# A decoder's block transposes by way of DRAM: one VectorE operation per 512 columns, 8 KB tiles, 2 KB stores, paired loads

## The chip, the core and the metric

The kernel runs on one core of a Trainium2 chip. The metric is the device time of one execution in microseconds (us), as the median of several runs. The engines are TensorE (PE; its weight loads, PEld, overlap the matmuls), VectorE (DVE), ScalarE (ACT), GpSimd (POOL) and SyncE (SP), which issues nearly all DMAs. SBUF is the on-chip memory with 128 partitions; PSUM holds the results of matmuls; DRAM is the memory outside.

## The reference

Six blocks are added to a residual stream `x` of 4 batches x 512 tokens x 512 features, each on the layernorm of `x`:

```python
x = x + L0_attn(layernorm(x))           # 16 heads of 32, one shared key and value head
x = x + L0_xattn(layernorm(x), ctx)     # mixes features with softmax(q k^T) of the context
x = x + L0_ffn(layernorm(x))            # 4-bit weights, width 1408, SiLU gate, then RMS norm
x = x + L1_attn(layernorm(x))           # 16 heads of 32
x = x + L1_xattn(layernorm(x), ctx)     # 16 heads of 128, 8 key/value heads, 512 keys
x = x + L1_ffn(layernorm(x))            # 32 slots of rank 16, the top 2 are gated
```

`L1_xattn` is the part that the change touches most. For each batch and head:

```python
scores = q @ k.T / sqrt(128)            # 512 x 512
attn   = softmax(where(mask, scores, -inf))
out    = attn @ v                       # then all heads' outputs times Wo
```

All is float32. The kernel keeps that precision with three matmuls of a high and a low part for each product (`three`): a value is split into a rounded `h` tile and the rest, an `l` tile.

## The kernel before

The stages follow one another, each with its own period: L0 (attention), X0 (mixing), FF, L1 (attention), X1 (cross-attention, 64 heads) and R1 (the routed part). Later stages' loads and layernorms begin while earlier stages run.

No instruction is issued as it is written. `Recorder` notes every operation as a task with the tiles that it reads and writes; `put` and `after` give it a place in a rough order. Then `arrange` (line 327) plans all tasks with `run`, a list scheduler that has a cost for each operation, DMA queues, PSUM banks and numbered buffers for every pool. It goes forward and backward `ROUNDS` times, and of the `ROUNDS + 1` forward plans keeps the shortest by its own costs. Some tasks may go to either of two engines: `split_sbuf` (line 704) puts the rounded copy on ScalarE or VectorE and the subtraction on GpSimd or VectorE, and `run` decides which. The instructions are then issued in the planned order, all from line 1845, and each engine keeps its order. So all profile rows of the planned work have L1845, and only the tiles' names tell them apart.

Two pools of SBUF matter here. `tp_` holds `TBUFS` = 50 tiles of 2 KB per partition (tag `t`), `wp` holds `WBUFS` = 17 tiles of 4 KB (tag `w`), for weights and for stacked operands.

`block_turn(tiles, got)` (line 756) transposes a matrix of 512 x 512 that lies in four tiles of 128 x 512. It has three parts:

- `turn(t)`: VectorE transposes tile `t` in blocks of 32 x 32 (`tr<-pe` in X1, `tr<-h` for layernorms). It takes two operations of 256 columns, each into one of two 4 KB tiles `tr` from `wp`.
- `away(j)`: SP stores half `j`, in four DMAs of 32 partitions, to a DRAM buffer `turn` (`turn<-tr`). The pieces are 512 bytes long.
- `back(k)`: SP loads one chunk of 128 columns, 256 KB, in pieces of 2 KB, into a tile `pt` of `tp_` (`pt<-turn`), and `split_sbuf` makes `turnedh` and `turnedl` from it for TensorE.

In X1 each of the 64 heads makes its scores with TensorE (`kTh`, `qh` and the like), VectorE moves them out of PSUM with the mask and their row minimum (`pe`, `nmc`), ScalarE takes the exponential, `pe` is scaled, `block_turn` turns the four `pe` tiles, and TensorE weighs the values with `turnedh` and `turnedl` (`vh`, `vl`). The same helper turns the normalised `h` tiles of 15 layernorms: four each in FF, L1 and X1, three in R1. The others are transposed by TensorE.

The functions that the diff touches and what calls them:

Of the kernel before, what the change touches and what calls it, by code (L numbers as in the profile page):

```python
# [10 lines left out]
F32 = mybir.dt.float32  # L11
# [10 lines left out]
P = 128  # L22
NB = 4
S = 512
D = 512
QT = S // P
KC = D // P
NH = 16
HD = 32
HG = P // HD  # L30
# [7 lines left out]
LN_EPS = 1e-5  # L38
RMS_EPS = 1e-6
BIG = 1e30  # L40
TBUFS = 50
WBUFS = 17
START = 45.0
DQ = 50.0
PER_L0, PER_X0, PER_F1, PER_L1, PER_X1, PER_R1 = 16.5, 12.5, 6.1, 22.5, 11.7, 25.0
# [9 lines left out]
WG = 2  # L55
OUT1 = 3.0
UM, UE, UH, UL = 0, 0, 0, 0
ROUNDS = 16

KEEP = 0, 1, 0, 1, 1, 2  # L60
TRACE = []
# [7 lines left out]
DT = 6  # L69
# [257 lines left out]
def arrange(tasks):  # L327
# [8 lines left out]
    best = None  # L336
    for n in range(ROUNDS + 1):
        done = run(tasks, False)
        span = max(t.end for t in done)
        TRACE.append(round(span, 1))  # L340
        if best is None or span < best[0]:
            best = span, done, [(t.start, t.end, t.engine, t.calls) for t in done], [
                (tile, tile.slot) for t in done for tile in t.tiles
            ]
        if n == ROUNDS:
            break
# [202 lines left out]
def decoder_kernel(ctx: ExitStack, tc: tile.TileContext, a: dict, out: bass.AP):  # L549
# [8 lines left out]
    nc = Recorder()  # L558
    PSUM = bass.MemoryType.PSUM

    def pool(name, bufs, n=None, **k):
        return Pool_(ctx.enter_context(tc.tile_pool(name=name, bufs=bufs or 1, **k)), bufs, n or name)

    base = pool("base", None)
    small = pool("small", 4)
    wp = pool("weights", WBUFS)
    tp_ = pool("tiles", TBUFS)
    dram = pool("scratch", None, space=bass.MemoryType.DRAM)
    ps = pool("ps", 1, space=PSUM)

# [29 lines left out]
    n = 2 * NI * KC  # L600
# [31 lines left out]
    def T(dt=F32, shape=(P, S), name="t"):  # L632
        return tp_.tile(list(shape), dt, tag="t", name=name)

    def pair(shape=(P, S), name="p"):
        return T(F32R, shape, name + "h"), T(F32R, shape, name + "l")
# [19 lines left out]
    def at(pr, *ix):  # L656
        return pr[0][ix], pr[1][ix]
# [46 lines left out]
    def split_sbuf(pr, src, dt, act=False):  # L704
        hi, lo = pr
        after(dt, lambda: copy(hi, src, *(("scalar", "vector") if act else ("vector", "scalar"))))
        after(dt + 0.8, lambda: join(lo, src, f32(hi), ALU.subtract, "gpsimd", "vector"))
# [4 lines left out]
    def add_to_x(t, src):  # L712
        nc.vector.tensor_tensor(x[:, t, :], x[:, t, :], src, ALU.add)
# [16 lines left out]
    def weight(t, key, src, cols=None, keep=False):  # L730


        got = {}

        def load():
            if key in stored:
                got["w"] = wp.tile(stored[key].tile.shape, F32R, tag="w", name="w")
                nc.sync.dma_start(f32(got["w"]), f32(stored[key]))
            else:
                got["w"] = split_weight(key, src, cols, keep, act=ACT_JIT and keep)  # L740

        put(t, t, [load])
        if keep and key[0] in EARLY:
            early.append((key, src, cols))

        def parts(sl=ALL, flat=False):
            if flat:
                return got["w"][:, sl]
            return got["w"][:, 0, sl], got["w"][:, 1, sl]

        return parts

    def chunks(w):
        return w.rearrange("(c p) o -> p c o", p=P)

    def block_turn(tiles, got):


        tr, dr = [None] * 2, [None] * 2

        def turn(t):
            for j in range(2):
                if t == 0:
                    tr[j] = wp.tile([P, 2 * S], F32, tag="w", name="tr")
                nc.vector.transpose(
                    tr[j].rearrange("p (b t i) -> p b t i", t=QT, i=HD)[:, :, t, :],
                    tiles[t][:, j * 2 * P : (j + 1) * 2 * P].rearrange("p (b i) -> p b i", i=HD),
                )

        def away(j):  # L770
            dr[j] = dram.tile([2, P, HG, P], F32, tag="turn", name="turn", bufs=DT)
            for n in range(HG):
                nc.sync.dma_start(
                    dr[j][:, :, n, :].rearrange("c (q j) n -> j (c q) n", j=HD),
                    tr[j][n * HD : (n + 1) * HD, :].rearrange("j (b n) -> j b n", n=P),
                    run=4 * P,
                )

        def back(k):
            pt = T(name="pt")  # L780
            nc.sync.dma_start(pt, dr[k // 2][k % 2].rearrange("p a n -> p (a n)"))
            got[k] = pair(name="turned")
            split_sbuf(
                [g.rearrange("p (t a i) -> p a t i", t=QT, a=HG) for g in got[k]],
                pt.rearrange("p (a t i) -> p a t i", t=QT, a=HG),
                3.5,
                True,
            )

        return (  # L790
            [lambda t=t: turn(t) for t in range(QT)],
            [lambda j=j: away(j) for j in range(2)],
            [lambda k=k: back(k) for k in range(KC)],
        )

    def layernorm_T(t0, t1, b, on_act=0, blocks=False, pool=False):
# [44 lines left out]
        if blocks:  # L841
            turns, aways, backs = block_turn(st["h"], st["hT"])
            put(n, t1, turns)
            put(t1, t1 + 0.2, aways)
            put(t1 + 4, t1 + 5, backs)
        else:
            put(n, t1, [lambda c=c: turn(c) for c in range(KC)])
# [200 lines left out]
    for b in range(NB):  # L1048
        t0 = T_X0 + b * PER_A0
        cT = context(t0 - 6, b)  # L1050
        u = {"qk": [None] * 2, "at": [None] * QT}

        def both(pq, j, u=u, b=b):
            u["qk"][j] = pair(name="qk")
            split(u["qk"][j], pq, cols[:, 5 + j : 6 + j], 1.3, b < SP)

        for j in range(2):
# [3 lines left out]
                lambda k, j=j: wx(slice(k * 2 * P + j * P, k * 2 * P + (j + 1) * P)),  # L1061
                cT,
                CC,
                lambda pq, j=j, both=both: both(pq, j),
# [35 lines left out]
    for b in range(NB):  # L1100
# [27 lines left out]
        for c in range(KC):  # L1128
            t0 = now + (4 * b + c) * per
            u = {}  # L1130

            def queries(pq, u=u, c=c):
# [7 lines left out]
                lambda k, c=c: wq0[k](slice(c * P, (c + 1) * P)),  # L1140
# [255 lines left out]
    for i in range(NI):  # L1396
        t = DQ + (ff0 + NI * per - 45 - DQ) * i / NI
# [12 lines left out]
    for b in range(NB):  # L1410
# [23 lines left out]
        for k in range(QT):  # L1434
# [5 lines left out]
                lambda c, k=k, hT=hT, wv=wv: (at(hT[c], ALL, tok(k)), wv[c]()),  # L1440
                lambda pv, k=k, f=values: f(pv, k),
            )
        oT = []
        for c in range(KC):
            t0 = now + (4 * b + c) * per
            u = {}
            for j in range(2):
                n0 = j * D + c * P
                w = weight(
                    t0 - (A1 + 0.5 - 0.2 * j) * per,  # L1450
                    ("qk1", j, c),
                    chunks(a["wqkv1"][:, n0 : n0 + P]),
                    KC,
                    keep=True,
                )

                def turned(pq, j=j, c=c, u=u):
# [13 lines left out]
                    lambda k, w=w: w(slice(k * P, (k + 1) * P)),  # L1471
# [5 lines left out]
            def normalise(w, pd, c=c, oT=oT):  # L1477
# [18 lines left out]
                lambda h, k, v=v, c=c: v[k][:, (4 * c + h) * HD : (4 * c + h + 1) * HD],  # L1496
# [10 lines left out]
        for t in range(QT):  # L1507
# [5 lines left out]
                lambda c, t=t, oT=oT, wo=wo: (at(oT[c], ALL, tok(t)), wo[c]()),  # L1513
                lambda po, t=t, b=b: add_to_x(b * QT + t, po),
# [6 lines left out]
    for b in range(NB):  # L1521
# [12 lines left out]
        for g in range(4):  # L1534
# [21 lines left out]
            for j in range(2):  # L1556
# [3 lines left out]
                    lambda k, j=j, wk=wk: wk(slice(k * 2 * XH + j * XH, k * 2 * XH + (j + 1) * XH)),  # L1560
                    cT,
                    CC,
                    lambda pk, j=j, f=keyed: f(pk, j),
# [21 lines left out]
            for i in range(4):  # L1585
# [9 lines left out]
                u = {"pe": [None] * QT, "pT": [None] * QT}  # L1595

                def queries(pq, u=u):
# [6 lines left out]
                    lambda k, w=wq: w(slice(k * P, (k + 1) * P)),  # L1604
# [21 lines left out]
                def scale(t, u=u):  # L1626
# [4 lines left out]
                    scaled_by(pe, pe, rec[:, t % 2 : t % 2 + 1], "vector", "scalar")  # L1631

                turns, aways, backs = block_turn(u["pe"], u["pT"])

                def weigh(k, u=u, kv=kv, i=i, oT=oT):
# [98 lines left out]
    for b in range(NB):  # L1734
        t0 = now + b * per
        hT = layernorm_T(t0 - 2.1 * per, t0 - 1.5 * per, b, NA["R1"], b in DV["R1"])
        u = {"gu": [None] * QT, "gT": [None] * KC}
# [193 lines left out]
```

## Time and profile before

| What | Value |
|---|---|
| Median of 3 runs | 2060.33 us (2054.5 to 2066.38) |
| The profiled execution: its own time | 2058.85 us |
| The profiled execution: its span | 2057.1 us |
| TensorE clock granted, mean | 0.993 |
| Busy: PE, DVE, ACT, POOL | 96%, 90%, 60%, 58% of the span |
| DMA on SP's queue | 349472 packets, 465.50 MB, 72.7% of 16 engines' span |
| Stores `turn<-tr` | 632, 128 KB each |
| Loads `pt<-turn` | 316, 256 KB each |
| VectorE transposes | 632 of 128 x 256 (512 of `pe`, 120 of `h`) |

The profile is one execution seen by the hardware profiler. A group of instructions is given with its tiles, its shape, its count, its busy time, the mean length of one in ns, and the engine's idle time just before them with what ended it. The chain of waits follows the work that ended last back to the start, at each step to what released it. SPq is SP's queue of DMA issues. The DMA share is the mean busy share of the 16 DMA engines.

### The profile page before, as it was taken

To read this page: it belongs to the slowest core of one execution; us is meant where nothing else is said; L and a number is where in the kernel's file an instruction comes from. 1 tells how busy PE (TensorE), PEld (TensorE's weight loads), DVE (VectorE), ACT (ScalarE), POOL (GpSimd) and SP (SyncE) were. 2 spreads that over 40 slices of the span, in tenths; PEclk is the share of its full clock that TensorE was granted. 3 is DMA by queue.
4 is the path that set the end of the run, shared out by engine and by line. 5 is a ranking of instruction groups with operands and counts; after the bars stand their busy time and mean duration, and the time that the engine had idled before them with its cause. 6 is when DMAs were issued, how large, how long until landed. Compare 5 with 4: busy or idle time off the path is not lost.

```text
span 2057.1 us, 31942 instructions
## 1 busy us (share of the span) xinstructions
PE 1984.3 (96%) x9728; PEld 1476.8 (72%) x9728; DVE 1848.7 (90%) x3645; ACT 1239.2 (60%) x2461; POOL 1195.0 (58%) x930
## 2 busy tenths in 40 slices
PE   7999999999999999999999999999999999999999
PEld 6755554778877856565656777787888777887677
DVE  8999998999999889898899898999999889998883
ACT  5876767467757355454546767676666557555520
POOL 5688889378777466867577445454454244233610
PEclk9999999999999999999999999999999999999999
DMA  7554444656758777777764889999999899988911
GB/s 254 198 187 149 144 159 145 232 185 231 261 171 296 222 229 240 211 243 221 222 169 141 246 236 272 288 288 294 299 299 304 246 307 292 317 255 247 273 60 58
DMA packets 350075, 467.57 MB, mean 227 GB/s; under 512 B 28944, under 2 KB 211472, under 8 KB 349904
## 3 DMA queue, kind: packets, MB, share of 16 engines
q1 hardware_dynamic: 349472, 465.50, 72.7%
q8 instruction: 77, 1.26, 0.3%
q14 instruction: 94, 0.77, 0.1%
q10 hardware_dynamic: 432, 0.04, 0.0%
HBM read 291.36 MB, written 173.93 MB: 226 GB/s over the span
## 4 chain that ended last, share of the span: by engine, by line
PE 65%; DVE 12%; DMA 12%; ACT 5%; issue 2%; SPq 2%; POOL 1%; ACTq 0%; DVEq 0%; POOLq 0%
PE mm L1845 65%; DMA pt<-turn 6%; DVE pe L1845 2%; SPq L1845 2%; DVE tr L1845 2%; DMA stack<-stack 2%; DVE nm L1845 2%; DMA turn<-tr 2%; ACT pT L1845 1%; DMA stack<-ql 1%; DVE x L1845 1%; ACT turnedh L1845 1%; ACT pe L1845 1%; DVE ol L1845 1%; DVE ql L1845 1%
## 5 line engine op out<-in xcount | busy, mean ns | idle before, releaser
L1845 POOL TENSOR_TENSOR turnedl<-pt,turnedh 128x512 fp32r<-128x512 f32 x249 | 328.8, 1334 | 407.2 <-ACT turnedh L1845 181.7
L1845 PE MATMUL mm<-turnedh,w 128*128 128x512 f32 x1120 | 414.6, 398 | 7.8 <-ACT turnedh L1845 3.0
L1845 DVE TENSOR_REDUCE nm<-mm 128x1 f32<-128x512 f32 x512 | 323.3, 678 | 35.3 <-PE mm L1845 34.5
L1845 PE MATMUL mm<-stack 96*128 96x512 f32 (+1 forms) x1024 | 325.8, 422 | 25.6 <-DMA stack<-stack 17.7
L1845 ACT ACTIVATE pT<-mm 128x512 f32<-128x512 f32 x512 | 273.2, 609 | 78.9 <-PE mm L1845 70.4
L1845 POOL TENSOR_TENSOR acc<-acc,pT 128x512 f32<-128x512 f32 x200 | 271.0, 1378 | 31.5 <-DVE acc L1845 12.6
L1845 PEld LDWEIGHTS mm<-stack 96*128 96x128 f32 (+1 forms) x1024 | 186.1, 192 | 140.5 <-issue 35.4
L1845 PE MATMUL mm<-turnedl,w 128*128 128x512 f32 x736 | 282.8, 394 | 1.2 <-POOL turnedl L1845 1.2
L1845 PEld LDWEIGHTS mm<-turnedh,w 128*128 128x128 f32 x1120 | 211.2, 189 | 65.7 <-ACT gu L1845 7.8
L1845 ACT ACTIVATE pe<-pe,nmc 128x512 f32<-128x512 f32 x256 | 184.6, 722 | 112.6 <-DVE nmc L1845 105.9
L1845 ACT CAST turnedh<-pt 128x512 fp32r<-128x512 f32 x291 | 176.5, 617 | 113.5 <-DMA pt<-turn 105.7
L1845 PE MATMUL mm<-w,oh 128*128 128x512 f32 x640 | 203.9, 391 | 5.6 <-ACT oh L1845 5.6
L1845 POOL TENSOR_TENSOR acc<-pT 128x512 f32<-128x512 f32 x118 | 155.6, 1333 | 77.2 <-ACT pT L1845 60.9
L1845 DVE STREAM_TRANSPOSE tr<-pe 128x256 f32<-128x256 f32 x512 | 198.3, 419 | 2.2 <-ACT pe L1845 2.0
L1845 DVE CUSTOM_DVE_ANT_0 pe<-mm,mb 128x512 f32<-128x512 f32 x256 | 169.7, 670 | 4.9 <-PE mm L1845 4.3
L1845 POOL TENSOR_TENSOR w<-ws,w 128x512 fp32r<-128x512 f32 x93 | 126.0, 1364 | 70.1 <-ACT w L1845 41.2
L1845 PEld LDWEIGHTS mm<-turnedl,w 128*128 128x128 f32 x736 | 139.1, 189 | 26.5 <-POOL turnedl L1845 2.7
L1845 ACT ACTIVATE gu<-mm,scales 128x512 f32<-128x512 f32 x173 | 113.5, 691 | 57.5 <-PE mm L1845 56.8
L1845 PEld LDWEIGHTS mm<-w,oh 128*128 128x128 f32 x640 | 118.9, 188 | 32.1 <-ACT oh L1845 8.0
L1845 POOL TENSOR_TENSOR gu<-gu 128x512 f32<-128x512 f32 x83 | 109.7, 1333 | 44.4 <-DVE gu L1845 33.0
L1845 DVE SCALAR_TENSOR_TENSOR gu<-mm,scales,gu 128x512 f32<-128x512 f32 x176 | 122.1, 738 | 2.4 <-PE mm L1845 2.3
L1845 PE MATMUL mm<-w,ol 128*128 128x512 f32 x320 | 123.7, 391 | 0.0
(235 smaller groups left out, 4543.9 us busy)
## 6 DMA issues: line engine op xcount, KB each, us to landing
turn<-tr SPq DMA_DIRECT2D x632, 128.0 KB
pt<-turn SPq DMA_DIRECT2D x316, 256.0 KB
w<-scr SPq DMA_DIRECT2D x148, 512.0 KB
stack<-stack SPq DMA_DIRECT2D x96, 384.0 KB
scr<-w SPq DMA_DIRECT2D x56, 512.0 KB
stack<-qh SPq DMA_DIRECT2D x96, 256.0 KB
w<-gu SPq DMA_DIRECT2D x44, 512.0 KB
w<-dn SPq DMA_DIRECT2D x44, 384.0 KB
```

What stands on the lines that cost most here:

```text
L1845: got = getattr(getattr(real, t.engine), name)(*[made(v) for v in a_], **{n: made(v) for n, v in k.items()})
```

## The change

`turn` makes one operation of 512 columns into one 8 KB tile `tr`, from a new pool `big` of two buffers. `away` stores it in four DMAs of 256 KB with pieces of 2 KB. `back` loads two chunks at a time, 512 KB in pieces of 1 KB, into a 4 KB tile of `wp`, and splits each chunk from its half. For the room of `big`, `tp_` goes to 44 tiles and `wp` to 16. `ROUNDS` goes from 16 to 32. `run=` tells the planner the length of the pieces. Every computed value stays the same.

```diff
-TBUFS = 50
-WBUFS = 17
+TBUFS = 44
+WBUFS = 16
+BBUFS = 2
...
-ROUNDS = 16
+ROUNDS = 32
...
+    big = pool("big", BBUFS)
...
     def block_turn(tiles, got):
-        tr, dr = [None] * 2, [None] * 2
+        u = {}
 
         def turn(t):
-            for j in range(2):
-                if t == 0:
-                    tr[j] = wp.tile([P, 2 * S], F32, tag="w", name="tr")
-                nc.vector.transpose(
-                    tr[j].rearrange("p (b t i) -> p b t i", t=QT, i=HD)[:, :, t, :],
-                    tiles[t][:, j * 2 * P : (j + 1) * 2 * P].rearrange("p (b i) -> p b i", i=HD),
+            if t == 0:
+                u["tr"] = big.tile([P, KC * S], F32, tag="b", name="tr")
+
+            nc.vector.transpose(
+                u["tr"].rearrange("p (e c t i) -> p c e t i", e=HG, c=KC, t=QT)[:, :, :, t, :],
+                tiles[t].rearrange("p (c e i) -> p c e i", c=KC, e=HG),
+            )
+
+        def away(n):
+            if n == 0:
+                u["dr"] = dram.tile([P, HG, KC * P], F32, tag="turn", name="turn", bufs=DT)
+            nc.sync.dma_start(
+                u["dr"][:, n, :].rearrange("(e j) s -> j e s", j=HD),
+                u["tr"][n * HD : (n + 1) * HD, :].rearrange("j (e s) -> j e s", e=HG),
+                run=4 * S,
+            )
+
+        def back(k):
+            if k % 2 == 0:
+                u["pt"] = wp.tile([P, HG, 2 * P], F32, tag="w", name="pt")
+                nc.sync.dma_start(
+                    u["pt"], u["dr"][:, :, k * P : (k + 2) * P], run=8 * P
                 )
-
-        def away(j):
-            dr[j] = dram.tile([2, P, HG, P], F32, tag="turn", name="turn", bufs=DT)
-            for n in range(HG):
-                nc.sync.dma_start(
-                    dr[j][:, :, n, :].rearrange("c (q j) n -> j (c q) n", j=HD),
-                    tr[j][n * HD : (n + 1) * HD, :].rearrange("j (b n) -> j b n", n=P),
-                    run=4 * P,
-                )
-
-        def back(k):
-            pt = T(name="pt")
-            nc.sync.dma_start(pt, dr[k // 2][k % 2].rearrange("p a n -> p (a n)"))
             got[k] = pair(name="turned")
             split_sbuf(
                 [g.rearrange("p (t a i) -> p a t i", t=QT, a=HG) for g in got[k]],
-                pt.rearrange("p (a t i) -> p a t i", t=QT, a=HG),
+                u["pt"][:, :, k % 2 * P : (k % 2 + 1) * P].rearrange("p a (t i) -> p a t i", t=QT),
                 3.5,
                 True,
             )
...
-            [lambda j=j: away(j) for j in range(2)],
+            [lambda n=n: away(n) for n in range(HG)],
```

## The prediction

> **What bounds the kernel now.** I read the whole page first, then the busy time by stage, the chain of waits, the groups by shape and the issuing queue. All work issued through the recorder carries the one line L1845, so I go by tile names. First the page's shares:
>
> ```profile
> span 2057.1 us, 31942 instructions
> PE 1984.3 (96%) x9728; PEld 1476.8 (72%) x9728; DVE 1848.7 (90%) x3645; ACT 1239.2 (60%) x2461; POOL 1195.0 (58%) x930
> ```
>
> TensorE is the bound as a mean; VectorE stands close behind. The changed helper, `block_turn`, works 64 times in the stage X1 (about 1110 to 1960 us) and 15 times for layernorms elsewhere, so X1 is read for itself (columns: stage, its length, then busy time and count of PE, PEld, DVE, ACT, POOL, the granted clock, the DMA share, GB/s):
>
> ```profile
> 1110.00:1960.00 850.00, 824.93 (x3731) 666.12 (x3728) 774.37 (x1880) 543.86 (x1144) 391.23 (x298) 1.00 0.92 276
> 1300.00:1500.00 200.00, 196.06 (x890) 159.21 (x889) 189.11 (x457) 137.46 (x290) 101.33 (x77) 1.00 0.97 296
> ```
>
> TensorE sits idle for 25 us of the 850, at full clock. Matmuls overlap, so busy time hides thin gaps. In the timeline two 128x512 matmuls in a row take 0.61 us where one takes 0.39, a step of 0.22 to 0.23; two 128x256 take 0.40 where one takes 0.28, a step of 0.12. The groups from 1150 to 1900 hold 2972 of the first and 347 of the second: 2972 x 0.226 + 347 x 0.115 = 712 us of 750. So 38 us of slack at most (less if records are missing): X1 can gain 25 to 40 us. The chain of waits, cut to X1, says where the slack lies:
>
> ```profile
> by line: PE mm L1845 51.6%; DMA pt<-turn 12.9%; DVE pe L1845 5.6%; SPq L1845 4.7%; DVE tr L1845 4.4%; DMA turn<-tr 4.2%; issue 2.9%; ACT pe L1845 1.8%; ACT turnedh L1845 1.8%; DVE turnedl L1845 1.0%; DVE x L1845 1.0%; POOL turnedl L1845 0.9
> ```
>
> The path of the turned blocks (transposes, store issues, stores, loads) holds 4.4 + 4.7 + 4.2 + 12.9 = 26% of the chain. One passage of it, in order of time (start, length, what):
>
> ```profile
> 1199.90 1.59 SPq L1845
> ...
> 1201.54 2.44 DMA turn<-tr
> ...
> 1204.17 3.22 DMA pt<-turn
> ...
> 1207.41 0.62 ACT turnedh L1845
> ```
>
> SP issues stores one behind the other, the last store lands, the load that waited for it lands, and the copies begin. The rows priced below:
>
> ```profile
> L1845 DVE STREAM_TRANSPOSE tr<-pe 128x256 f32<-128x256 f32 x512 | 198.3, 419 | 2.2 <-ACT pe L1845 2.0
> L1845 DVE TENSOR_TENSOR turnedl<-pt,turnedh 128x512 fp32r<-128x512 f32 x67 | 72.6, 1085 | 24.2 <-ACT turnedh L1845 21.5 <-DMA turn<-tr 1.3 <-issue 1.2
> L1845 ACT ACTIVATE pT<-mm 128x512 f32<-128x512 f32 x512 | 273.2, 609 | 78.9 <-PE mm L1845 70.4 <-DVE s L1845 6.8 <-ACT w L1845 0.3
> L1845 SPq DMA_DIRECT2D turn<-tr x632: 302/463/1592, 390.1 to 1954.1; - x158
> L1845 SPq DMA_DIRECT2D pt<-turn x316: 319/424/2095, 396.6 to 1957.2; - x158
> ```
>
> **The change, part by part.**
>
> *Transposes.* 632 of 128x256 become 316 of 128x512, a shape that the trace has not. Two of 419 ns are 838, the upper end. The scaled subtraction takes 460 ns on 128x256 and 740 on 128x512, so 256 more elements cost 280: 419 + 280 = 700, which I take; a TENSOR_REDUCE over 512 takes 678, the lower end. Gain 316 x 0.138 = 44 us of VectorE (0 to 50). On X1's chain the transposes are 4.4% x 850 = 37 us; 0.138/0.838 of that is -6.
>
> But the planner spends it again. The built program puts 113 subtractions `turnedl` on VectorE (67 before), 49 copies `turnedh` (25), and 142 scalings of `pe` (166): 46 x 1.085 + 24 x 0.613 - 24 x 0.668 = +49 us. VectorE as a whole is not relieved; GpSimd is, by 46 x 1.334 = 61 us it did not need.
>
> *Issues on SP.* Stores 632 to 316, loads 316 to 158. At 0.463 and 0.424 us that is 146 + 67 = 213 us less of issuing. In the built program a DMA also waits for the one that used its completion semaphore eight issues earlier, so fewer and larger DMAs wait less often. X1's chain has 4.7% x 850 = 40 us of SP; twelve issues per turn become six: -20 (-10 if half of these pieces are of weights).
>
> *Stores in 2 KB pieces.* Between 60 and 300 us, where the rows moved have mostly 2 KB and more, 161 GB/s took a share of 0.50: 20.1 bytes per ns and engine. From 1300 to 1500, 0.97 x 16 x 200 = 3104 engine-us moved 59.2 MB. Some 16 heads store 16.8 MB of it in 512 B pieces; the other 42.4 MB at 20.1 cost 2109, so the stores took 995, 17 bytes per ns. At the rate of the long rows they take 836: -16%, or 5% of the stage's DMA time. On the chain (4.2%, 36 us) that is -6 at best, against a last store of 256 KB instead of 128, 0.43 us more at 296 GB/s, on about a dozen landings: +5. I take 0.
>
> *Loads of two chunks, in 1 KB pieces.* No row moves mainly 1 KB pieces; they lie between the two rates, so loads get 0 to 18% dearer and the stage's DMA share changes by between -5 points and none. For the copies that wait, the first chunk of a pair lands with the second: 256 KB more, 0.86 us at 296 GB/s. X1's chain has 110 us of these landings, some 24 of 4 to 5 us. Were all first chunks: +21; were all last: 0. I take +10, the middle, since first and second chunks are equally many.
>
> The Trainium skill, "DMA: Bandwidth & Descriptors", section "Why small descriptors are slow (HBM only)", gives each packet about 3 cycles beside one per 32 bytes. By that (an estimate from the page) a byte in 512 B pieces costs 19/16, in 1 KB 35/32, in 2 KB 67/64 cycles: stores -12%, loads +4.5%, which would put the share near 0.95. The same page, "Anatomy of one DMA", says that the semaphore fires only when the last byte is confirmed; this speaks against the change, whose first load waits for the whole 1 MB where it waited for half. The trace's landing of 2.44 us behind the last store fits; no row splits it.
>
> *Two 8 KB buffers.* A new wait: the first transpose of a turn waits for the four stores of the turn before the last. In the built program mostly 20 to 35 VectorE instructions of X1 (850/1880 = 0.45 us each) lie between that turn's last transpose and this one, 9 to 16 us; four issues and a landing are 4 x 0.46 + 2.4 to 5 = 4 to 7 us. So it is covered: 0. With the cover gone, the score evictions `pe<-mm` queue behind the transpose, their PSUM banks stay full and TensorE stops: at 1 us for each of 64 turns, 64 us.
>
> *Pools.* Six 2 KB tiles and one weight buffer fewer. In X1 the turned chunks leave the tile pool, so little is lost. From 60 to 1100 us TensorE idles 240 - 237.2 + 800 - 770.9 = 32 us; I price 12% fewer tiles at 12% more idle, +4, of the bounds 0 and +32 (idle doubled). X1's -16 is 0.25 us a turn; the eight layernorm turns there give back -2.
>
> *32 passes.* The planner keeps the best of 33 plans, not 17; every engine's order changes throughout. No row prices that: -10 to +10, taken as 0.
>
> Sum: -6 - 20 + 0 + 10 + 4 - 2 = -14 us; the parts' ends in X1 reach from -6 - 20 - 6 = -32 to -6 - 10 + 5 + 21 = +10. The profiled execution took 2058.85 us (span 2057.1), the median of the three runs is 2060.33, 1.5 more. From the median: 2046 us, with 2028 to 2050 as that case's own range. What comes next when the path shortens is TensorE itself, 25 to 40 us below.
>
> **Rivals.**
>
> *Nothing gained.* The turn path shortens at the issues and lengthens at the landings, and VectorE, as busy as before (91% in X1), sets the pace. For it: the 49 us given back, and DVE `pe` with 5.6% of X1's chain. Also, in the built order the matmuls between a head's last score and its first weighing grow from 24.4 to 27.1 us of steps: the planner found the turn longer, not shorter. Against: SP's part is certain. -6 - 10 + 0 + 10 + 4 = about -2: 2058.
>
> *Slower: the smaller tile pool.* X0, L0, FF and L1 run half the span and hardly use the turn, but plan with 44 tiles. Where a writer finds no free tile it comes late and TensorE waits. Idle doubled there is +32; with X1's -16: +16, 2076. It decides once the idle outside X1 grows by half, 16 us. Against it: ACT `pT`, the greatest user of tiles, waited 70.4 of its 78.9 us for TensorE and hardly for a tile's earlier readers.
>
> **How the numbers follow.** The gain has 0.45: 26% of X1's chain lies on the path cut, but the landings' sign is open. Nothing gained has 0.25, slower 0.30, since two prices that I set near nothing (pools, cover of the two buffers) can only go one way. About 0.5%, 10 us, is what a measurement of this kernel can tell from no change. The range goes from 2026 (all X1 ends and a little from the plan) to 2076 (the slower rival's price).
>
> **What would show it.** Right: X1 shorter by 10 to 20 us; SPq near 2.5% of X1's chain; transposes near 700 ns; VectorE's total within 20 us of 1849; DMA share in X1 at 0.87 to 0.92. Wrong: transposes of 800 ns or more; VectorE idle before `tr` on DMA `turn<-tr`, over 10 us; pt<-turn above 15% of X1's chain; or the stages before 1110 us longer by more than 10 us.

## The result and the profile after

The changed kernel took 2087.01 us as the median of four runs (2084.08 to 2088.25), beside 2060.26 us for the kernel before: 1.0135 times as long, with a 95% interval of 1.0115 to 1.0155. It is slower by 27 us, or 1.35%, and lies outside the predicted range of 2026 to 2076. The profiled execution took 2088.25 us.

The page's first lines of the changed kernel:

```profile
span 2086.5 us, 31002 instructions
PE 1998.5 (96%) x9728; PEld 1485.4 (71%) x9728; DVE 1856.2 (89%) x3366; ACT 1235.9 (59%) x2465; POOL 1138.5 (55%) x889
```

VectorE's total moved by 7.5 us, and GpSimd lost 56 us. All the planned work now has line L1850. Where the 29.4 us between the two spans went is read from the last matmul of each stage. The rows are those of one tile's instructions: shortest, median and longest in ns, then from when to when. `pT,v` ends the stage L1, `turnedh,vh` ends X1. Before:

```profile
L1845 PE MATMUL mm<-pT,v x1024: 592/592/618, 92.7 to 1103.8; 128*32 128x512 f32 x171
L1845 PE MATMUL mm<-turnedh,vh x256: 387/389/504, 1138.4 to 1947.1; 128*128 128x512 f32 x128
```

After:

```profile
L1850 PE MATMUL mm<-pT,v x1024: 592/592/1062, 90.6 to 1116.4; 128*32 128x512 f32 x171
L1850 PE MATMUL mm<-turnedh,vh x256: 387/389/632, 1154.2 to 1976.3; 128*128 128x512 f32 x128
```

L1 ends 12.6 us later. X1, from there to its last matmul, took 859.9 us instead of 843.3: 16.6 us more, where 10 to 20 less was predicted. The rest up to the span's end is unchanged (110.0 and 110.2 us). So there are two losses: one in stages that hardly use the changed helper, and one inside X1. These three numbers (end of L1, length of X1, rest) are given for every experiment below. The kernel before and one with the same order of all instructions (the first experiment) differed between their profiles by 5.4 us at the end of L1 (1103.8 and 1098.4) and by 5.1 us in the length of X1 (843.3 and 838.2), so smaller differences in either say nothing.

X1 after, by the columns of the prediction's windows (PE, PEld, DVE, ACT, POOL, granted clock, DMA share, GB/s):

```profile
1110.00:1960.00 850.00, 817.53 (x3687) 658.29 (x3687) 767.47 (x1595) 537.54 (x1146) 341.71 (x258) 0.99 0.85 269
```

And the chain of waits in the same stretch:

```profile
by line: PE mm L1850 25.9%; DMA pt<-turn 15.9%; DMA turn<-tr 14.0%; SPq L1850 6.3%; DVE pe L1850 5.9%; DVE tr L1850 5.1%; issue 4.2%; DMA ws<-in_xwo 3.2%; DMA ws<-in_xwq 2.9%; DVE turnedl L1850 2.5%; DMA w<-scr 1.7%; DVE ql L1850 1.2%; ACT 
```

The reader is to see the landings of the stores, `turn<-tr`: 4.2% of the chain before, 14.0% now. SPq rose from 4.7% to 6.3% though it issues half as many DMAs of the turn, and matmuls fell from 51.6% to 25.9%. Every engine was busy for less of the 850 us, and the DMA share fell from 0.92 to 0.85: X1 has more waiting in it, not more work. SP itself, by what it waited for in this stretch (us in total, times, longest), before:

```profile
SPq L1845 <- DMA turn<-tr: 28.3, 49, 2.0
```

and after:

```profile
SPq L1850 <- DMA turn<-tr: 152.8, 95, 7.0
```

One such wait in SP's timeline of the changed kernel:

```profile
1410.11 2.75 SPq L1850 DMA_DIRECT2D turn<-tr  x4
1421.07 1.20 SPq L1850 DMA_DIRECT2D pt<-turn  x2
1422.37 3.80 SPq L1850 DMA_DIRECT2D turn<-tr  x4
1426.27 1.59 SPq L1850 DMA_DIRECT2D ws<-in_xwq  x1
```

and the same stretch in the chain:

```profile
1412.08 8.97 DMA turn<-tr
...
1421.07 4.05 DMA pt<-turn
...
1425.19 0.63 ACT turnedh L1850
1425.82 0.07 issue
1425.89 0.38 POOL turnedl L1850
1426.27 4.87 DMA ws<-in_xwq
1431.14 0.02 issue
1431.16 0.63 ACT w L1850
```

The four stores are issued by 1412.86. The next instruction on SP is a load that needs all of them, and SP issues nothing for 8.2 us, until they have landed (7.0 us is the longest single wait that the trace puts down to `turn<-tr`). In the passage shown of before the landing took 2.44 us and the load's 3.22. The DMA engines were not idle meanwhile: SP had issued two loads of 512 KB at 1408.08 and a store of 512 KB at 1409.43, which with the four stores makes 2.6 MB. At the 280 GB/s moved from 1408 to 1421 us that is about 9.4 us (an estimate from these rows), so most of the 13 us up to the landing is the queue of transfers itself.

Behind the load on SP stand the next turn's stores and a weight load, `ws<-in_xwq`, that has nothing to do with the turn. SP reaches the weight load at 1426.17 (1422.37 + 3.80). The chain puts its last release down to GpSimd's `turnedl`, which itself needs this load's data. The weight is what `w` on ScalarE, the next in the chain, waits for. Over the whole stretch ScalarE's `w` waited for another weight as follows (us in total, times, longest), before:

```profile
ACT w L1845 <- DMA ws<-in_xwo: 4.8, 6, 2.0
```

and after:

```profile
ACT w L1850 <- DMA ws<-in_xwo: 26.2, 16, 4.8
```

### The profile page after: what moved, and what is told of

Its sections match the earlier page's. It is cut to its first block, busy times and chain, and to the rows that moved or that the text cites. A ratio compares the mean times of both kernels' runs of the same rounds, so it can differ in the third digit from the quotient of the medians.

```text
span 2086.5 us, 31002 instructions
## 1 busy us (share of the span) xinstructions
PE 1998.5 (96%) x9728; PEld 1485.4 (71%) x9728; DVE 1856.2 (89%) x3366; ACT 1235.9 (59%) x2465; POOL 1138.5 (55%) x889
## 4 chain that ended last, share of the span: by engine, by line
PE 35%; DMA 20%; DVE 10%; ACT 3%; SPq 3%; issue 2%; POOL 1%; DVEq 0%; ACTq 0%; POOLq 0%
PE mm L1850 35%; DMA pt<-turn 7%; DMA turn<-tr 6%; SPq L1850 3%; DVE pe L1850 2%; DVE tr L1850 2%; DMA ws<-in_xwo 1%; DMA ws<-in_xwq 1%; DVE turnedl L1850 1%; DMA stack<-ql 1%; DMA stack<-stack 1%; DMA w<-scr 1%; DMA cst<-in_ctxT 1%; ACT turnedh L1850 1%; ACT pT L1850 1%
## 5 line engine op out<-in xcount | busy, mean ns | idle before, releaser
L1850 POOL TENSOR_TENSOR turnedl<-pt,turnedh 128x512 fp32r<-128x512 f32 x203 | 271.1, 1343 | 398.2 <-ACT turnedh L1850 217.2
L1850 PE MATMUL mm<-turnedh,w 128*128 128x512 f32 x1120 | 411.9, 397 | 5.3 <-ACT turnedh L1850 2.7
L1850 DVE TENSOR_REDUCE nm<-mm 128x1 f32<-128x512 f32 x512 | 323.8, 678 | 40.3 <-PE mm L1850 39.0
L1850 PE MATMUL mm<-stack 96*128 96x512 f32 (+1 forms) x1024 | 328.0, 423 | 25.2 <-DMA stack<-max 6.4
L1850 ACT ACTIVATE pT<-mm 128x512 f32<-128x512 f32 x512 | 274.7, 613 | 95.3 <-PE mm L1850 88.4
L1850 PEld LDWEIGHTS mm<-stack 96*128 96x128 f32 (+1 forms) x1024 | 187.7, 194 | 137.7 <-ACT pT L1850 37.9
L1850 PE MATMUL mm<-turnedl,w 128*128 128x512 f32 x736 | 282.9, 393 | 2.3 <-POOL turnedl L1850 2.1
L1850 POOL TENSOR_TENSOR acc<-acc,pT 128x512 f32<-128x512 f32 x197 | 263.5, 1358 | 31.8 <-DVE acc L1850 10.7
L1850 PEld LDWEIGHTS mm<-turnedh,w 128*128 128x128 f32 x1120 | 210.6, 189 | 61.8 <-ACT gu L1850 7.7
L1850 ACT ACTIVATE pe<-pe,nmc 128x512 f32<-128x512 f32 x256 | 184.2, 720 | 109.2 <-DVE nmc L1850 108.2
L1850 ACT CAST turnedh<-pt 128x512 fp32r<-128x512 f32 x267 | 154.9, 618 | 128.6 <-DMA pt<-turn 122.2
L1850 PE MATMUL mm<-w,oh 128*128 128x512 f32 x640 | 205.9, 394 | 12.2 <-ACT oh L1850 11.2
L1850 POOL TENSOR_TENSOR acc<-pT 128x512 f32<-128x512 f32 x118 | 156.3, 1338 | 81.0 <-ACT pT L1850 63.1
L1850 POOL TENSOR_TENSOR w<-ws,w 128x512 fp32r<-128x512 f32 x95 | 128.7, 1360 | 131.2 <-ACT w L1850 96.7
L1850 DVE STREAM_TRANSPOSE tr<-pe 128x512 f32<-128x512 f32 x256 | 177.3, 696 | 1.1 <-DMA turn<-tr 0.5
L1850 DVE CUSTOM_DVE_ANT_0 pe<-mm,mb 128x512 f32<-128x512 f32 x256 | 169.4, 672 | 3.9 <-PE mm L1850 3.7
L1850 DVE TENSOR_TENSOR turnedl<-pt,turnedh 128x512 fp32r<-128x512 f32 x113 | 139.9, 1238 | 27.5 <-ACT turnedh L1850 22.9
L1850 PEld LDWEIGHTS mm<-turnedl,w 128*128 128x128 f32 x736 | 138.8, 189 | 30.0 <-POOL turnedl L1850 3.7
L1850 PEld LDWEIGHTS mm<-w,oh 128*128 128x128 f32 x640 | 118.7, 188 | 43.8 <-ACT oh L1850 14.7
L1850 ACT ACTIVATE gu<-mm,scales 128x512 f32<-128x512 f32 x175 | 115.0, 691 | 43.5 <-PE mm L1850 42.7
L1850 POOL TENSOR_TENSOR gu<-gu 128x512 f32<-128x512 f32 x85 | 112.6, 1334 | 49.4 <-DVE gu L1850 30.5
L1850 DVE SCALAR_TENSOR_TENSOR gu<-mm,scales,gu 128x512 f32<-128x512 f32 x176 | 122.4, 737 | 5.1 <-PE mm L1850 3.6
```

The source lines that it names most:

```text
L1850: got = getattr(getattr(real, t.engine), name)(*[made(v) for v in a_], **{n: made(v) for n, v in k.items()})
```

## The experiments

The theories at the outset: (A) the load pair waits on SP for the whole 1 MB and holds up what is queued behind it; (B) the smaller pools make the earlier stages later; (C) the plan, by 32 passes, is another and worse one; (D) the pieces of the loads, 1 KB, are dear. They do not exclude one another; the two places of the loss called for at least two causes. Runs of one study share their runs of the kernel before, so all times stand as ratios.

### The search alone

```diff
-ROUNDS = 16
+ROUNDS = 32
```

> The kernel before with 32 passes of the search and nothing else. Theory Q (queue): in X1 SP holds each pair of loads until the last of four 256 KB stores has landed, and what stands behind it on SP comes late; that gives about 17 of the 27 us. Theory P (pools): 44 and 16 buffers give the 11 us by which the last L1 weighing came later (1113 against 1101 us). Theory S (search): the plan is another one, and any new plan moves the time by 10 to 25 us. Q and P: 2060 within 6 us. S: more than 10 us away from 2060, in either direction.

Measured: 0.9995 times before (0.9977 to 1.0012). The built order is the same, instruction for instruction: the longer search found nothing that it holds for better. Its profile (L1 ends at 1098.4, X1 838.2, rest 109.4) shows by how much one plan differs between executions.

The converse, the changed kernel with `ROUNDS = 16`:

> The changed kernel with 16 passes of the search. The search keeps the shortest of its plans, so the plan is the same or one that counted as longer. Theory S (plans differ on the chip by 10 us and more without regard to their counted length): more than 8 us from 2087 in either direction if the plan differs. Theories Q and P: within 8 us of 2087, last L1 weighing again near 1116, X1 again over 852.

Measured: 1.0104 (1.0073 to 1.0135), L1 at 1111.9, X1 854.6, rest 109.7. Here the plan is another one, and 32 passes did not help: the plan that is shortest by the planner's own costs was no shorter on the chip. That it was longer isn't shown, since the intervals overlap. With 16 passes 21 us of the loss are there still (2076.47 beside 2055.63), so (C) can be a small part at most.

### The pools

The kernel before with the pools of the changed one:

```diff
-TBUFS = 50
-WBUFS = 17
+TBUFS = 44
+WBUFS = 16
```

> The kernel before with TBUFS 44 and WBUFS 16 and nothing else (16 passes). Theory P: 2070 to 2076, the last L1 weighing near 1112 us. Theory Q: 2058 to 2065, and SP waits for turn<-tr in X1 near 28 us as before. Theory S: any place from 2045 to 2085.

Measured: 1.0112 (1.0077 to 1.0148). L1 ends at 1121.5, X1 takes 848.3, the rest 109.0. Most of the loss, 17.7 of the span's 21.7 us, is ahead of X1. Then each pool alone:

> The kernel before with TBUFS 44 alone (WBUFS 17, 16 passes). If the six 2 KB tiles are what delays the stages before X1 when both pools shrink (last L1 weighing at 1121 us against 1104): 2070 to 2080, last L1 weighing over 1112. If the weight pool's one tile is: 2052 to 2062, last L1 weighing under 1108.

> The kernel before with WBUFS 16 alone (TBUFS 50, 16 passes). If the weight pool's one tile delays the stages before X1: 2066 to 2080, last L1 weighing over 1112. If the six tiles do: 2052 to 2062, last L1 weighing under 1108.

Measured: six tiles fewer 1.016 (1.0142 to 1.0179), one weight buffer fewer 1.0156 (1.014 to 1.0171); L1 ends at 1129.8 and 1127.2, X1 takes 847.8 and 849.2, the rest 108.8 and 109.7. Both times lie above the ranges expected. Either edit alone costs at least what both cost together, so the sizes do not add. Each is a new plan, and a plan scatters. In all three kernels with the old helper and smaller pools X1 is 4.5 to 5.9 us longer than before as well, which is hardly more than the scatter. FF's end and L1 (PE, PEld, DVE, ACT, POOL, clock, DMA share, GB/s) before:

```profile
740.00:1115.00 375.00, 358.51 (x1817) 228.14 (x1816) 337.88 (x491) 191.37 (x367) 278.38 (x216) 0.98 0.69 211
```

with 44 tiles:

```profile
740.00:1115.00 375.00, 352.35 (x1766) 226.16 (x1765) 321.21 (x481) 190.69 (x371) 264.85 (x208) 0.97 0.69 212
```

with 16 weight buffers:

```profile
740.00:1115.00 375.00, 352.52 (x1754) 223.13 (x1754) 329.78 (x486) 190.16 (x370) 260.41 (x205) 0.98 0.69 213
```

TensorE does 51 and 63 matmuls fewer in the same 375 us. No engine is busier, and the DMA traffic is the same: the work comes later. And the pools the other way round, on the kernel of the next section, `TBUFS = 50` and `WBUFS = 13`:

> The one-operation kernel with the old stores and loads and with TBUFS 50, WBUFS 13, BBUFS 2: the two 8 KB buffers are paid for by the weight pool alone, which no longer holds the turned blocks. If the 44 tiles are what cost 12 us before X1 (last L1 weighing at 1116 against 1104 us): last L1 weighing at 1100 to 1107, time 2040 to 2055, below both kernels. If the weight pool is the tight one: 2065 or more, with the loss before X1.

Measured: 1.0213 (1.017 to 1.0256), L1 at 1152.4, X1 829.3, rest 112.6. Six more tiles did not make up for three fewer weight buffers: L1 ends 36.6 us later than in the kernel of the next section. Over all runs, the kernels with 44 tiles and 16 weight buffers end L1 between 1111.9 and 1121.6 us (one further down, with a faulty plan, at 1127.7), those with 50 and 17 between 1098.4 and 1108.8. So (B) holds for the loss ahead of X1, though the two groups are only 3.1 us apart where they come closest, and the 12.6 us are one plan's. At which stage a plan loses them differs: by the last `mm<-ident,oT` the kernel before with the new pools ended L0 at 370.2 us (367.7 before), the changed kernel at 381.7, so that all its loss lies there. Why there isn't settled. From 60 to 380 us, before:

```profile
60.00:380.00 320.00, 315.66 (x1778) 190.18 (x1777) 298.42 (x487) 232.37 (x456) 261.24 (x204) 1.00 0.50 163
```

After:

```profile
60.00:380.00 320.00, 306.70 (x1718) 185.38 (x1717) 293.50 (x475) 228.29 (x446) 256.50 (x201) 0.98 0.49 157
```

### One operation, the old transfers

The changed kernel's pools, `big`, 32 passes and the one transpose of 512 columns, with the old eight stores and four loads:

```diff
-        def away(n):
...
+        def away(j):
+            dr = u["dr", j] = dram.tile([2, P, HG, P], F32, tag="turn", name="turn", bufs=DT)
+            for n in range(HG):
+                nc.sync.dma_start(
+                    dr[:, :, n, :].rearrange("c (q j) n -> j (c q) n", j=HD),
+                    u["tr"][n * HD : (n + 1) * HD, j * 2 * S : (j + 1) * 2 * S].rearrange("j (b n) -> j b n", n=P),
+                    run=4 * P,
+                )
...
+            pt = T(name="pt")
+            nc.sync.dma_start(pt, u["dr", k // 2][k % 2].rearrange("p a n -> p (a n)"))
```

> The changed kernel (pools, two 8 KB buffers, one VectorE operation for 512 columns, 32 passes), but its stores and loads as before: eight stores of 128 KB in 512 B pieces, four loads of 256 KB that each wait for their half. Theory Q: X1 back to its length of before (first score to last weighing 830 us, 848 in the changed kernel), SP waits for turn<-tr in X1 under 50 us, time 2065 to 2072. Theory P alone: time 2070 to 2076 if X1 is not the pools' doing, 2087 if it is. Theory S: within 10 us of 2087 or not, without regard to SP's waits.

Measured: 1.0031 (1.0005 to 1.0057); L1 at 1115.8, X1 841.2, rest 108.0; SP waits 21.2 us for `turn<-tr`. So X1's loss is gone as soon as the old transfers are back, and the loss ahead of X1 stays. That places one cause in the stores and loads.

### The whole wait

The last kernel with one edit: four stores of 256 KB in the old pieces of 512 B, so that each single load waits for all four.

```diff
-        def away(j):
-            dr = u["dr", j] = dram.tile([2, P, HG, P], F32, tag="turn", name="turn", bufs=DT)
+        def away(n):
+            if n == 0:
+                u["dr"] = dram.tile([KC, P, HG, P], F32, tag="turn", name="turn", bufs=DT)
```

> The one-operation kernel with single loads as before, but four stores of 256 KB (512 B pieces), each over all four chunks, so that every load waits for the whole 1 MB. Theory Q: SP's waits for turn<-tr in X1 rise from 20 to over 100 us, X1 from 841 to over 850, time 2070 to 2085. Theory W: X1 within 5 us of 841, time 2058 to 2068.

Measured: 1.0185 (1.0153 to 1.0216), so 1.5% over the kernel that it was made from. L1 ends at 1117.8, X1 takes 849.7, 8.5 more, and the rest 124.6, 16.6 more. So this kernel, whose loads each wait for the whole turn, is slower without any pairing or new pieces. But SP waits only 43.7 us for the stores, where over 100 was expected, and the larger part of the loss fell behind X1: in its place the experiment is a miss.

The other way, the changed kernel's pieces with the wait cut in half, was tried first:

```diff
+        def away(j):
+            dr = u["dr", j] = dram.tile([P, HG, 2 * P], F32, tag="turn", name="turn", bufs=DT)
+            for n in range(HG):
+                nc.sync.dma_start(
+                    dr[:, n, :].rearrange("(e j) s -> j e s", j=HD),
+                    u["tr"][n * HD : (n + 1) * HD, :].rearrange("j (e s) -> j e s", e=HG)[
+                        :, :, j * 2 * P : (j + 1) * 2 * P
+                    ],
+                    run=8 * P,
+                )
...
+                    u["pt"], u["dr", k // 2]
```

> The changed kernel, but stored by halves: eight stores of 128 KB in 1 KB pieces, and each pair's load (512 KB, 4 KB pieces) waits for its own half only. Theory Q: SP waits for turn<-tr in X1 fall from 153 to under 80 us and the time to 2072 to 2080. Theory P: 2084 to 2090, X1 as long as in the changed kernel. Theory S: no relation between SP's waits and the time.

Measured: 1.0482 (1.0456 to 1.0508), L1 at 1127.7, X1 895.5, rest 124.4. It decides nothing. By the planner's code, the slice of a strided view makes it count every store with the whole 8 KB row, twice its bytes, so the plan rests on wrong costs; how much of the 4.8% that explains wasn't tried. SP's wait for the stores did fall to 1.4 us.

The clean pair lays the DRAM buffer out by halves of 256 columns, so that no slice is needed. First the changed kernel's plan, instruction for instruction, with stores in 1 KB pieces and loads in 4 KB pieces, and the whole wait:

```diff
-                u["dr"] = dram.tile([P, HG, KC * P], F32, tag="turn", name="turn", bufs=DT)
+                u["dr"] = dram.tile([2, P, HG, 2 * P], F32, tag="turn", name="turn", bufs=DT)
...
-                    u["pt"], u["dr"][:, :, k * P : (k + 2) * P], run=8 * P
+                    u["pt"], u["dr"][k // 2], run=8 * P
```

> The changed kernel with its own plan (every engine's order is the same, instruction for instruction), but another layout in DRAM: stores in 1 KB pieces (2 KB in the changed kernel), loads in 4 KB pieces (1 KB). Theory N: the pieces set the time: by the rates 17 and 20 bytes per ns stores get dearer by up to 10% and loads cheaper by up to 18%, the time moves by 5 us or more, down if the loads count. Theories Q and W: 2087 within 4 us.

Measured: 1.0112 (1.0079 to 1.0146), X1 851.4, L1 at 1119.3, rest 109.5. X1 is 8.5 us shorter than in the changed kernel, but the ratio's interval meets that kernel's 1.0115 to 1.0155. So (D) is a small part at most. Then the same pools, operation, pieces and paired loads, with eight stores of half a turn each, so that a load pair waits for its half only:

```diff
-        def away(n):
-            if n == 0:
-                u["dr"] = dram.tile([2, P, HG, 2 * P], F32, tag="turn", name="turn", bufs=DT)
+        def away(j):
+            dr = u["dr", j] = dram.tile([P, HG, 2 * P], F32, tag="turn", name="turn", bufs=DT)
```

> The kernel with paired loads that wait for their half (eight stores), in exactly the same order on every engine, but with stores in 1 KB pieces (512 B there) and loads in 4 KB pieces (2 KB there). Theory Q (the wait for the whole 1 MB is the loss, the pieces are not): 2045 to 2058, X1 824 to 832, and the 2152 us of the first kernel with these pieces was its plan, in which each store was counted with twice its bytes. Theory N (pieces): over 2075.

Measured: 0.9983 (0.997 to 0.9995), X1 824.7, L1 at 1113.4, rest 109.2. The two differ by 27 us in X1 and by 1.3% in time. The last matmul of X1 with the whole wait:

```profile
L1850 PE MATMUL mm<-turnedh,vh x256: 388/389/504, 1157.1 to 1970.7; 128*128 128x512 f32 x128
```

with the half wait:

```profile
L1850 PE MATMUL mm<-turnedh,vh x256: 387/389/503, 1149.0 to 1938.1; 128*128 128x512 f32 x128
```

SP's waits from 1110 to 1960 us with the whole wait:

```profile
SPq L1850 <- DMA turn<-tr: 143.8, 92, 6.3
```

with the half wait:

```profile
SPq L1850 <- DMA turn<-tr: 61.7, 99, 1.8
```

and the chains of that stretch, whole wait:

```profile
by line: PE mm L1850 37.6%; DMA pt<-turn 12.7%; DMA turn<-tr 11.1%; DVE pe L1850 5.6%; DVE tr L1850 5.3%; issue 3.8%; SPq L1850 3.6%; DVE turnedl L1850 2.8%; DMA ws<-in_xwq 2.3%; ACT pe L1850 2.0%; ACT turnedh L1850 1.5%; DMA ws<-in_xwo 1.3
```

half wait:

```profile
by line: PE mm L1850 57.3%; DMA pt<-turn 9.3%; DMA turn<-tr 5.1%; SPq L1850 5.0%; DVE pe L1850 3.4%; DVE tr L1850 3.1%; issue 2.8%; ACT pe L1850 2.1%; DVE turnedl L1850 1.7%; DMA ws<-in_xwo 1.3%; ACT turnedh L1850 1.1%; DMA w<-scr 1.0%; POO
```

SP waits as often, but the longest wait falls from 6.3 to 1.8 us, and the chain is TensorE's again. ScalarE's `w` waits 4.6 us for `ws<-in_xwo`, and 23.4 with the whole wait. (A) holds: with the whole wait X1 is about 27 us longer. The number of stores (four of 256 KB, eight of 128 KB) and the plan differ between the two as well, and the planner was told other lengths of pieces (`run=`) in each, so the 27 us are the price of the wait with what goes with it.

### Did the planner not see it?

The planner puts the loads where it believes the stores to have landed. The changed kernel, with each store to `turn` told to land 2.5 us later:

```diff
+LATE = 2.5
+        t.late = LATE if name == "dma_start" and outs and outs[0].tile.key == ("scratch", "turn") else 0.0
...
-                t.end = max(t.end, queues[q] + READ + TAIL * t.delay)
+                t.end = max(t.end, queues[q] + READ + TAIL * t.delay + t.late)
```

> The changed kernel, but the planner is told that a store to the turn buffer lands 2.5 us later than it counts. Theory Q, if the loss is that SP stands before loads which were planned too early, with other transfers behind them: SP's waits for turn<-tr in X1 fall from 148 to under 70 us, X1 from 860 to under 850, time 2065 to 2080. If the loss is the longer turn itself (the data come later whatever is issued meanwhile): time 2083 to 2095, though SP waits less.

Measured: 1.0138 (1.0105 to 1.017), no gain in the time. Inside X1 it does what the first theory expected: SP waits 55.3 us for the stores instead of 152.8, and X1 takes 832.2 us, 27.7 less. Number, size, pieces and whole wait of the transfers are the changed kernel's; only the plan is another. So X1's loss is not the price of these transfers as such: it goes with where the loads stand in SP's order, and it could be planned around. But the median of 2084 us lies in the second theory's range. L1 ends at 1121.6, 5.2 us later, and the rest takes 122.4, 12.2 us longer. Why the rest grew isn't shown; it is about as long in the kernel of single loads with the whole wait (124.6) and in the one with the faulty plan (124.4).

### Paired loads and their pieces

The kernel of old transfers, with the four loads made two of 512 KB in 2 KB pieces:

```diff
-            pt = T(name="pt")
-            nc.sync.dma_start(pt, u["dr", k // 2][k % 2].rearrange("p a n -> p (a n)"))
+            if k % 2 == 0:
+                u["pt"] = wp.tile([P, 2, S], F32, tag="w", name="pt")
+                nc.sync.dma_start(u["pt"], u["dr", k // 2].rearrange("c p a n -> p c (a n)"), run=4 * S)
```

> The one-operation kernel with the old stores (512 B pieces, by halves), but two chunks loaded at a time into a 4 KB tile of the weight pool (512 KB, 2 KB pieces). Theory W (weight pool): the pair holds a weight buffer from the load's start until its second chunk is split, weights come late; X1 (last L1 weighing to last X1 weighing) grows from 841 to over 852 us, time 2075 to 2100. Theory Q (each load waits for the whole 1 MB on SP): X1 stays within 5 us of 841, time 2058 to 2068. Theory N (length of the pieces): as Q, the pieces are the old ones.

Measured: 0.9997 (0.9979 to 1.0015); X1 828.4, 12.8 less than with single loads; L1 at 1115.7, rest 108.4. None of the three theories had expected a gain. The same edit on the kernel before, with its own pools, two operations and 16 passes:

> The kernel before (50 and 17 buffers, two operations of 256 columns into 4 KB tiles, 512 B stores by halves, 16 passes) with paired loads into a 4 KB tile of the weight pool and nothing else. If paired loads are what shortens X1 (828 us with them, 841 without, in the one-operation kernels) and the smaller pools what costs 12 us before it: last L1 weighing near 1104, X1 825 to 835, time 2040 to 2050, below both kernels. If the one operation per 512 columns is needed as well: X1 near 843, time 2055 to 2065.

Measured: 1.0002 (0.998 to 1.0024); X1 833.7, 9.6 less than before; L1 at 1108.5, rest 106.6. X1's gain is there in both profiles, but not in the ratio: part of it goes to the later end of L1, and no more can be said. At last this kernel's plan, instruction for instruction, with stores in 1 KB pieces and loads in 4 KB pieces:

```diff
-            dr[j] = dram.tile([2, P, HG, P], F32, tag="turn", name="turn", bufs=DT)
+            dr[j] = dram.tile([P, HG, 2 * P], F32, tag="turn", name="turn", bufs=DT)
...
-                pt[0] = wp.tile([P, 2, S], F32, tag="w", name="pt")
-                nc.sync.dma_start(pt[0], dr[k // 2].rearrange("c p a n -> p c (a n)"), run=4 * S)
+                pt[0] = wp.tile([P, HG, 2 * P], F32, tag="w", name="pt")
+                nc.sync.dma_start(pt[0], dr[k // 2], run=4 * S)
```

> The kernel before with its own pools and two operations of 256 columns, loads in pairs that wait for their half, stores in 1 KB and loads in 4 KB pieces; the order on every engine is that of the same kernel with 512 B and 2 KB pieces. If the pieces are worth what they were in the one-operation kernels (3 to 8 us): 2045 to 2053, X1 under 833, below both kernels. If not: 2052 to 2058.

Measured: 0.9958 (0.9945 to 0.9971), 2043.28 us beside 2052.61: faster than both kernels. X1 takes 821.0 us, L1 ends at 1108.8, the rest takes 107.6.

X1's window with 512 B stores and 2 KB loads:

```profile
1110.00:1960.00 850.00, 832.08 (x3794) 677.22 (x3793) 805.42 (x1926) 548.17 (x1164) 357.81 (x271) 1.00 0.91 277
```

with 1 KB stores and 4 KB loads:

```profile
1110.00:1960.00 850.00, 840.31 (x3856) 688.51 (x3856) 813.77 (x1958) 551.85 (x1170) 359.17 (x271) 1.00 0.87 277
```

The same plan, the same 277 GB/s, at a share of 0.87 instead of 0.91. In the other two pairs of equal plans X1 was shorter with the longer load pieces too, by 8.5 us (changed kernel against 1 KB and 4 KB) and by 3.7 us (2 KB against 4 KB loads, both with the half wait), but there the intervals of the ratios overlap, and the 3.7 us are within the scatter. Stores and loads were changed together, so which of them pays is not split. SP's total of waiting is no measure by itself: here it waits 94.8 us for the stores in 120 waits, of 3.6 us at most, and the landings are 2.4% of X1's chain.

## Why the prediction was wrong, step by step

**The sum** was -14 us; measured were +27 (29.4 between the two profiles). X1, forecast at -16, grew by 16.6 us, and the stages ahead of it, forecast at +2, by 12.6. The range "2028 to 2050" does not follow from the parts either: their upper end, +10, gives 2070. The 0.43 and 0.86 us count a KB as 1000 bytes (0.44 and 0.89 otherwise), which changes no term.

**The transposes** had the right length: 696 ns for 700. The operation waited 0.5 us in sum for a free buffer of `big`, so the cover of the two buffers holds:

```profile
L1850 DVE STREAM_TRANSPOSE tr<-pe 128x512 f32<-128x512 f32 x256 | 177.3, 696 | 1.1 <-DMA turn<-tr 0.5 <-ACT pe L1850 0.4
L1850 DVE TENSOR_TENSOR turnedl<-pt,turnedh 128x512 fp32r<-128x512 f32 x113 | 139.9, 1238 | 27.5 <-ACT turnedh L1850 22.9 <-issue 2.1 <-PE mm L1850 1.7
```

The gain of 44 us was not there in the busy time: before, 512 operations of 419 ns are 214.5 us, but the row's busy time is 198.3: their spans overlap. With the layernorms' it fell from 245.6 to 218.8 us, by 27. The give-back came to 50 us (`turnedl` +67, as one took 1238 ns and not 1085, `turnedh` +11, the scalings -28). That VectorE's total still moved by no more than 7.5 us is luck: its other rows fell by 16. The -6 on the chain doesn't show: `tr` holds 5.1% of X1's chain, 4.4% before.

**The issues on SP** (-20) failed twice over. The larger DMAs are dearer to issue:

```profile
L1850 SPq DMA_DIRECT2D turn<-tr x316: 303/650/2320, 402.6 to 1971.0; - x158
L1850 SPq DMA_DIRECT2D pt<-turn x158: 518/571/1963, 409.4 to 1977.2; - x158
```

By these medians 316 x 0.650 + 158 x 0.571 = 296 us against 427 before: 131 us less, not 213. And SP's waits for `turn<-tr` grew by 124 us in X1, all its waits there together by 80 (from 322 to 402, the sums of that view's rows). On X1's chain SP's issues hold 6.3% x 850 = 54 us, where 40 were to become 20. I counted issuing and not standing.

**The loads' term** (+10), with the 0 for the stores, is the step that failed most in X1. The +10 priced the pair alone: a first chunk lands with the second, 0.86 us later. For the other part of the edit, a load that waits for all four stores where it waited for half of them, the sum has no term. The stores' landing got +5, for a larger last store, against -6. That the first load waits for the whole 1 MB stands in the prediction as speaking against the change, but without a price: it was put at nothing without a reason.

The runs show two things in its place. The wait is served on SP, which keeps its order, so it holds up the next turn's stores and the weights too: the landings `turn<-tr` hold 14.0% x 850 = 119 us of X1's chain, 36 before, and in the clean pair X1 is 27 us longer with the whole wait than with the half wait. And the pairing, priced as a loss, is a gain of 10 to 13 us in X1 where each load waits for its half. X1's -16 was thus within reach (18.6 us shorter than before with the half wait and the new pools, 9.6 with the pairing alone), but not by the terms of the sum: these kernels issue 632 stores as before.

The Trainium skill, "DMA: Bandwidth & Descriptors", section "Anatomy of one DMA", which treats the DMAs that GpSimd issues, has the semaphore fire only when the last byte is confirmed. SP's DMAs show the standing until the landing, 8.2 us in the passage above; no run shows how much of it is the confirmation.

**The pieces.** The DMA share of 0.85 lies below the 0.87 to 0.92 predicted, partly since X1 moved less in the same time: 269 / (16 x 0.85) = 19.8 bytes per ns and engine, 276 / (16 x 0.92) = 18.8 before. By these figures the transfers did become about 5% cheaper, and X1 was longer all the same. The sign of the choice of pieces was open in the prediction; the runs have the best time with 1 KB stores and 4 KB loads, from longer pieces on both sides than before.

**The pools** (+4, bounds 0 and +32) cost 12.6 us before X1 in the changed kernel, and 17.7 in the kernel with that edit alone. The bound held, the value taken did not. Its reason was 12% fewer tiles at 12% more idle; but six tiles alone ended L1 26.0 us later, and one weight buffer alone, which had no term of its own, 23.4. Idle time was also the wrong measure: from 60 to 1100 us TensorE idled 37.6 us instead of 31.9, only 5.7 more, while L1 ended 12.6 later. The rival "slower" took idle outside X1 to grow by 16 us at least and X1 to gain 16; neither came. It named one of the two causes, and that it ends 11 us below the measured time is luck, since its X1 has the wrong sign.

**32 passes** were taken at 0. For the kernel before that is exact. For the changed one nothing outside the bound of 10 us is shown (1.0104 with 16 passes, 1.0135 with 32).

**A sign that was misread.** Under "nothing gained" I had noted that the planner's own order put 27.1 us of matmuls instead of 24.4 between a head's last score and its first weighing. The planner, which counts the whole wait, left 2.7 us more of work for the turn to hide behind; I let it speak for a rival only and left the sum as it was. Of the signs of being wrong that I had listed, two came in: `pt<-turn` at 15.9% of X1's chain, and the stages before 1110 us longer by more than 10. Of the signs of being right, X1's length, SPq's share and the DMA share failed; the transposes and VectorE's total held.

## What to carry to other kernels

Before you merge stores or loads of a round trip through DRAM, write down for each load which stores it waits for: with merged loads that wait for their half the stage was 10 to 13 us shorter here, and with loads that wait for everything 27 us longer than with those. On a queue that issues in order, price a longer wait by what stands behind it, not by the bytes that land later. Where SBUF is planned to the last buffer, a buffer taken for one stage can be paid for in others: here L1 ended 23 us later for one weight buffer of 17. The cheap run is the kernel before with only the pools changed.

## What was not expected of the hardware

The time to issue a load on SP depended on its pieces: 512 KB took 571 ns in 1 KB pieces (at the shortest 518), and 377 in 2 KB (359) and 338 in 4 KB pieces (319) in the two kernels with paired loads and the old pools. A 256 KB load in 2 KB pieces, before, took 424 (319). So the pair in 1 KB pieces is the only load whose shortest issue is far from the others. For the stores the shortest issue is 302 or 303 ns whatever the pieces, and the median goes by the size of the store: 463 ns (512 B pieces, before) and 445 (1 KB, half wait) for 128 KB, but 734 (512 B), 696 (1 KB) and 650 (2 KB, changed kernel) for 256 KB.

TensorE's granted clock from 60 to 380 us was mostly lower where TensorE was busy for less: 1.00 with 315.7 us before, 0.98 with 306.7 in the changed kernel, and 0.94 with 294.0 in the kernel with 13 weight buffers. The two do not go in step: it was 0.96 with 309.7 us in the one-operation kernel with the old transfers, and 0.99 with 309.2 in the fastest kernel. Which came first in these windows, the gaps or the clock, wasn't tried.
